# Attention weights of one of two source blocks on GpSimd instead of VectorE, with a new split of the squares

## The chip, the cores and the metric

The kernel runs on one core of a Trainium2 chip. The metric is the device time of one execution in microseconds (us). Each timed kernel ran several times, in rounds with the kernel before on the same chip. DVE is VectorE, ACT is ScalarE, POOL is GpSimd, PE is TensorE.

## The reference, cut to what matters

Four graph layers follow each other on 3327 nodes with 64 features. The change touches only the last one, a hyperbolic attention layer:

```
left = x_tan @ att_W[:D] + att_b
right = x_tan @ att_W[D:]
adj_att = jax.nn.sigmoid(left + right.T) * adj           # 3327 x 3327
x_local = _logmap(x[:, None, :], x[None, :, :], C)
support_t = jnp.einsum('ij,ijd->id', adj_att, x_local)
```

The kernel never builds `x_local`. For each pair (source, target) it needs a weight, (1 + tanh(.)) * adj, which is twice the sigmoid, and a scalar function of the distance, which it fits by a Gelu and the square of that Gelu plus a constant. Their product is contracted with the source nodes on PE.

## The kernel before

The layer goes over 26 pairs. A pair is two source blocks of 128 nodes (b = 0, 1) against half of the targets (HN = 1664). So a pair's tiles `gl` and `th` are 128 x 3328. `SQ` is the column at which the squares are divided between ACT (below it) and DVE (from it on).

```
SQ = HN + 512                                   # 2176
...
    def distances(n, k):        # half k of the columns of both blocks
        ...                     # 8 matmuls into the tiles pts[0], pts[1]
        for b in range(2):
            S.activation(gs[n][:, b, ...], pts[b], AF.Gelu, scale=-HA)
        S.activation(ths[n][:, k, :], leftb, AF.Tanh, bias=righth, scale=0.5)

    def squares(n):
        S.activation(gl[:, :SQ], gl[:, :SQ], AF.Square, bias=hg)
        V.scalar_tensor_tensor(gl[:, SQ:], gl[:, SQ:], 2 * HG, gl[:, SQ:], op0=OP.add, op1=OP.mult)

    def weights(n):
        th, a = ths[n], adjs.pop(n)
        for b in range(2):
            V.scalar_tensor_tensor(th[:, b, :], th[:, b, :], 1.0, a[:, b, :], op0=OP.add, op1=OP.mult)

    def products(n):
        for lo, hi, hd in ((0, HN, HD), (HN, SQ, HD), (SQ, 2 * HN, HD + HG * HG)):
            V.scalar_tensor_tensor(gl[:, lo:hi], gl[:, lo:hi], hd, th[:, lo:hi], op0=OP.add, op1=OP.mult)
    ...
    for n in range(-2, len(pairs)):
        if n >= 0: products(n)
        if 0 <= n + 1 < len(pairs): distances(n + 1, 1)
        if n >= 0: gather(n)                    # PE: accx, columns in four chunks of 416 a block
        if 0 <= n + 1 < len(pairs):
            weights(n + 1); load3(n + 3); squares(n + 1)
        if n + 2 < len(pairs):
            begin(n + 2); distances(n + 2, 0)
        if n >= 0: gather_p(n)                  # PE: accp
```

(Cut: helpers, the other layers, and the collection of a half.) Each engine takes its instructions in the order in which this loop issues them.

## Time and profile before

| | before |
|---|---|
| median of the first 3 runs | 920.91 us (920.04 to 924.06) |
| one pair of layer 3, steady | 8.63 us |
| DVE in the steady stretch | busy 80.00 of 80.00 us |
| ACT, POOL in that stretch | 76.34 us, 0 us |

The table is for a stretch of layer 3 in which nothing but the 26-pair loop runs. It is read from the busy times in that window, and the period is the distance between two equal instructions in the timeline. The prediction shows those lines. One view that it does not show is the timeline of ACT (start, length, engine, line, operation, shapes, count; idle time before it and what ended it):

```profile
696.47 1.62 ACT L818 ACTIVATE gl<-pt 128x832 f32<-128x832 f32 x2 [0.37 <-PE pt L810]
697.98 1.68 ACT L825 ACTIVATE th<-leftb,righth 128x1664 f32<-128x1664 f32 x1
```

The reader sees that ACT waits 0.37 us for PE's distances in each pair. PE in turn waits for ACT's Gelu before it may overwrite a distance tile.

### The profile page before, as it was taken

To read this page: it belongs to the slowest core of one execution; us is meant where nothing else is said; L and a number is where in the kernel's file an instruction comes from. 1 tells how busy PE (TensorE), PEld (TensorE's weight loads), DVE (VectorE), ACT (ScalarE), POOL (GpSimd) and SP (SyncE) were. 2 spreads that over 40 slices of the span, in tenths; PEclk is the share of its full clock that TensorE was granted. 3 is DMA by queue.
4 is the path that set the end of the run, shared out by engine and by line. 5 is a ranking of instruction groups with operands and counts; after the bars stand their busy time and mean duration, and the time that the engine had idled before them with its cause. 6 is when DMAs were issued, how large, how long until landed. Compare 5 with 4: busy or idle time off the path is not lost.

```text
span 920.6 us, 9670 instructions
## 1 busy us (share of the span) xinstructions
PE 720.2 (78%) x4043; PEld 339.6 (37%) x4043; DVE 519.6 (56%) x618; ACT 356.3 (39%) x361; POOL 9.5 (1%) x18
## 2 busy tenths in 40 slices
PE   0999998998953999505999999115899997699970
PEld 0644445443431444203444445112344442244420
DVE  4200025000189000796676675862899998899986
ACT  0000011000022000111666665012899995799961
POOL 1000000000000000000000002000000000000000
PEclk9999999999985999856999999556999997899995
DMA  8999930997000599500688610300465562445501
GB/s 274 378 379 429 404 122 21 384 359 275 0 1 0 209 385 373 221 0 1 253 330 310 243 53 1 151 3 10 149 223 176 197 222 80 159 159 217 200 24 22
DMA packets 25345, 170.22 MB, mean 185 GB/s; under 512 B 9165, under 2 KB 9293, under 8 KB 16077
## 3 DMA queue, kind: packets, MB, share of 16 engines
q1 hardware_dynamic: 21718, 168.88, 48.1%
q10 hardware_dynamic: 3575, 0.64, 0.4%
q8 instruction: 33, 0.54, 0.2%
q14 instruction: 19, 0.16, 0.1%
HBM read 168.40 MB, written 0.85 MB: 184 GB/s over the span
## 4 chain that ended last, share of the span: by engine, by line
PE 62%; DVE 19%; DMA 10%; issue 4%; ACT 3%; ACTq 1%; POOL 0%; SPq 0%; DVEq 0%; POOLq 0%
PE acc L261 28%; PE pt L799 9%; PE accx L870 8%; DMA adj<-in_adjT 6%; PE cnt L450 4%; PE cnt L458 4%; PE accp L885 3%; DMA res<-in_adjT 3%; PE pt L810 2%; DVE sq L86 1%; DVE gl L854 1%; PE lin L245 1%; ACT gl L818 1%; DVE n L88 1%; DMA w<-in_W 1%
## 5 line engine op out<-in xcount | busy, mean ns | idle before, releaser
L261 PE MATMUL acc<-adj,m_n 128*64 128x416 f32 x816 | 203.8, 523 | 9.4 <-DMA adj<-in_adjT 8.8
L261 PEld LDWEIGHTS acc<-adj,m_n 128*64 128x64 f32 x816 | 85.4, 138 | 109.7 <-issue 90.3
L261 PE MATMUL acc<-res,m_n 128*64 128x416 f32 x432 | 108.0, 523 | 22.8 <-DVE m_n L349 22.2
L466 ACT ACTIVATE w<-cnt,ebias 128x832 uint16<-128x832 f32 x104 | 93.4, 950 | 62.9 <-PE cnt L458 51.8
L278 DVE COPY m_t<-acc 128x416 f32<-128x416 f32 x12 | 6.2, 582 | 189.1 <-PE acc L261 189.1
L845 DVE SCALAR_TENSOR_TENSOR th<-th,adj 128x1664 f32<-128x1664 f32 x52 | 97.7, 1887 | 12.5 <-ACT th L825 12.4
L799 PE MATMUL pt<-xs 64*128 64x416 f32 x208 | 99.4, 559 | 5.4 <-ACT gl L818 5.4
L799 PE MATMUL pt<-xw,xs 64*128 64x416 f32 x208 | 100.5, 565 | 0.0
L854 DVE SCALAR_TENSOR_TENSOR gl<-gl,th 128x1664 f32<-128x1664 f32 (+2 forms) x78 | 97.6, 1305 | 0.0
L870 PE MATMUL accx<-gl,xd 128*64 128x416 f32 x416 | 83.2, 539 | 13.8 <-DVE gl L854 13.8
L818 ACT ACTIVATE gl<-pt 128x832 f32<-128x832 f32 x104 | 84.1, 861 | 24.3 <-PE pt L810 24.3
L825 ACT ACTIVATE th<-leftb,righth 128x1664 f32<-128x1664 f32 x52 | 87.6, 1685 | 0.0
L450 PE MATMUL cnt<-mask,tri 128*128 128x416 bf16 x208 | 70.8, 344 | 2.4 <-ACT w L466 1.0
L261 PEld LDWEIGHTS acc<-res,m_n 128*64 128x64 f32 x432 | 44.5, 138 | 68.4 <-issue 66.5
L261 PE MATMUL acc<-w,part 128*64 128x416 bf16 x624 | 66.1, 346 | 4.3 <-DVE part L413 4.3
L458 PE MATMUL cnt<-behind,ones 128*128 128x416 bf16 x192 | 65.1, 339 | 0.0
L476 DVE TENSOR_TENSOR behind<-behind,mask 128x3328 bf16<-128x3328 bf16 x23 | 43.5, 1892 | 36.0 <-PE cnt L458 36.0
L217 PE MATMUL tr<-ident,h_n 128*128 128x128 f32 x26 | 6.0, 423 | 62.4 <-DVE h_n L139 62.4
L836 ACT ACTIVATE gl<-gl,hg 128x2176 f32<-128x2176 f32 x26 | 54.8, 2106 | 0.0
L870 PEld LDWEIGHTS accx<-gl,xd 128*64 128x64 f32 x416 | 30.8, 141 | 62.1 <-DVE gl L854 33.4
L810 PE MATMUL pt<-rows_i,rows_j 64*128 64x416 bf16 x208 | 50.8, 347 | 0.0
L443 DVE TENSOR_SCALAR mask<-adj 128x3328 bf16<-128x3328 f32 x21 | 39.5, 1885 | 19.9 <-DMA adj<-in_adjT 13.3
(228 smaller groups left out, 645.4 us busy)
## 6 DMA issues: line engine op xcount, KB each, us to landing
adj<-in_adjT SPq DMA_DIRECT2D x89, 1664.0 KB
res<-in_adjT SPq DMA_DIRECT2D x9, 1664.0 KB
xn<-in_x SPq DMA_DIRECT2D x1, 832.0 KB
out<-w SPq DMA_DIRECT2D x2, 416.0 KB
ih<-in_wihT ACTq DMA_DIRECT2D x4, 48.0 KB
hh<-in_whhT ACTq DMA_DIRECT2D x4, 48.0 KB
w<-in_W ACTq DMA_DIRECT2D x4, 16.0 KB
attw<-in_att_W SPq DMA_DIRECT2D x1, 64.0 KB
```

The source lines that it names most:

```text
L261: T.matmul(acc[q][h * D : (h + 1) * D, :CH], lhsT=lhsT, rhs=rhs, start=first, stop=last)
L450: T.matmul(p[:, i, :CH], lhsT=tri, rhs=mask[:, i0 : i0 + CH], start=True, stop=behind is None,)
L458: T.matmul(p[:, i, :CH], lhsT=ones, rhs=behind[:, i0 : i0 + CH], start=False, stop=True,)
L466: S.activation(w, p[:, :, :CH], AF.Relu, bias=ebias, scale=-EXP_UNIT)
L799: T.matmul(pts[b][:, i, :CH], lhsT=xs[rs, c * P : (c + 1) * P], rhs=rhs[rs, q0 : q0 + CH], start=True, stop=False,)
L810: T.matmul(pts[b][:, i, :CH], lhsT=rows_j[rs, j0 : j0 + P], rhs=rows_i[rs, i0 : i0 + CH], start=False, stop=True,)
L818: S.activation(gs[n][:, b, 2 * k * CH : (2 * k + 2) * CH].rearrange("p (i n) -> p i n", i=2), pts[b][:, :, :CH], AF.Gelu, scale=-HA,)
L825: S.activation(ths[n][:, k, :], leftb[:, hf * HN : (hf + 1) * HN], AF.Tanh, bias=righth[:, kk : kk + 1], scale=0.5,)
L836: S.activation(gl[:, :SQ], gl[:, :SQ], AF.Square, bias=hg)
L845: V.scalar_tensor_tensor(th[:, b, :], th[:, b, :], 1.0, a[:, b, :], op0=OP.add, op1=OP.mult)
L854: V.scalar_tensor_tensor(gl[:, lo:hi], gl[:, lo:hi], hd, th[:, lo:hi], op0=OP.add, op1=OP.mult)
L870: T.matmul(acc[i // 2][(i % 2) * D : (i % 2 + 1) * D, :CH], lhsT=xd[:, c, b, :], rhs=gl[:, b, i * CH : (i + 1) * CH], start=first, stop=last,)
```

## The change

The intent is to take one of the two weights instructions off DVE, the full engine, and give it to POOL, which is idle. As DVE would then have room, part of the squares moves from ACT to DVE.

```
-SQ = HN + 512
+SQ = 1280
...
-        def weights(n):
-            th, a = ths[n], adjs.pop(n)
-            for b in range(2):
-                V.scalar_tensor_tensor(th[:, b, :], th[:, b, :], 1.0, a[:, b, :], op0=OP.add, op1=OP.mult)
+        def weights(n, b):
+            th, a = ths[n][:, b, :], adjs[n][:, b, :]
+            if b == 0:
+                G.tensor_scalar(th, th, 1.0, None, op0=OP.add)
+                G.tensor_mul(th, th, a)
+            else:
+                V.scalar_tensor_tensor(th, th, 1.0, a, op0=OP.add, op1=OP.mult)
+                adjs.pop(n)
...
-            for lo, hi, hd in ((0, HN, HD), (HN, SQ, HD), (SQ, 2 * HN, HD + HG * HG)):
+            for lo, hi, hd in ((0, SQ, HD), (SQ, 2 * HN, HD + HG * HG)):
...
-                weights(n + 1)
+                weights(n + 1, 1)
...
                 distances(n + 2, 0)
+                weights(n + 2, 0)
```

(Long lines are joined.)

More of the change, by code (lines that the diff above doesn't have):

```diff
@@ L839, in squares @@
             )
-        def weights(n):
-            th, a = ths[n], adjs.pop(n)
-            for b in range(2):
-                V.scalar_tensor_tensor(
-                    th[:, b, :], th[:, b, :], 1.0, a[:, b, :], op0=OP.add, op1=OP.mult
-                )
+        def weights(n, b):
[6 more added lines that the diff above has]
+                adjs.pop(n)
         def products(n):
```

## The prediction

> **What bounds the kernel now.** Layer 3 alone is changed, so I read the busy time per engine for a steady stretch of it, then the groups of that stretch by shape, then the timeline of VectorE and of ScalarE, then the chain of waits. The steady stretch first (columns: stretch, its length, busy us and instructions of each engine, granted clock, DMA share, GB/s):
>
> ```profile
> 660.00:740.00 80.00, 80.00 (x518) 34.52 (x519) 80.00 (x57) 76.34 (x66) 0.00 (x0) 1.00 0.57 203
> ```
>
> PE and DVE are busy for all of it, ACT for 95%, POOL not at all, at full clock. A busy PE is not a PE at its peak, so this row alone does not choose between PE and DVE. The groups by shape give the durations (busy us, mean ns of one, idle time before it):
>
> ```profile
> L845 DVE SCALAR_TENSOR_TENSOR th<-th,adj 128x1664 f32<-128x1664 f32 x18 | 33.9, 1887 | 0.0
> L825 ACT ACTIVATE th<-leftb,righth 128x1664 f32<-128x1664 f32 x19 | 32.0, 1685 | 0.0
> L818 ACT ACTIVATE gl<-pt 128x832 f32<-128x832 f32 x38 | 30.8, 861 | 3.7 <-PE pt L810 3.7
> ...
> L836 ACT ACTIVATE gl<-gl,hg 128x2176 f32<-128x2176 f32 x9 | 18.9, 2105 | 0.0
> L854 DVE SCALAR_TENSOR_TENSOR gl<-gl,th 128x1664 f32<-128x1664 f32 x10 | 18.8, 1883 | 0.0
> ...
> L854 DVE SCALAR_TENSOR_TENSOR gl<-gl,th 128x1152 f32<-128x1152 f32 x10 | 13.5, 1349 | 0.0
> ...
> L837 DVE SCALAR_TENSOR_TENSOR gl<-gl 128x1152 f32<-128x1152 f32 x9 | 12.2, 1351 | 0.0
> ...
> L854 DVE SCALAR_TENSOR_TENSOR gl<-gl,th 128x512 f32<-128x512 f32 x10 | 6.8, 682 | 0.0
> ```
>
> Every DVE group has no idle time before it: DVE is back to back. The timeline of DVE gives the period (start, length):
>
> ```profile
> 689.19 3.77 DVE L845 SCALAR_TENSOR_TENSOR th<-th,adj 128x1664 f32<-128x1664 f32 x2
> 692.88 1.35 DVE L837 SCALAR_TENSOR_TENSOR gl<-gl 128x1152 f32<-128x1152 f32 x1
> 694.15 3.75 DVE L854 SCALAR_TENSOR_TENSOR gl<-gl,th 128x1664 f32<-128x1664 f32 x3
> 697.82 1.88 DVE L845 SCALAR_TENSOR_TENSOR th<-th,adj 128x1664 f32<-128x1664 f32 x1
> ```
>
> One pair takes 697.82 - 689.19 = 8.63 us. The six durations are 2 x 1.887 + 1.351 + 1.883 + 0.682 + 1.349 = 9.04 us, so neighbours overlap by (9.04 - 8.63)/6 = 0.07 us. DVE is the full engine, and there are 26 pairs: 224 us of the 921.
>
> The chain of waits shows how near the others are:
>
> ```profile
> 694.39 1.94 PE pt L799 x8
> 696.34 0.27 PE pt L810
> 696.60 2.96 PE accx L870 x16
> ```
>
> The chain runs along PE all the time. PE's own work per pair is two distance halves of 1.95, the gather of 2.96 and the accp products of 1.51: 8.37 us. The second distance half takes 2.2 us instead of 1.95, because its second tile waits for ScalarE's Gelu. ACT steps in 4 x 0.75 + 2 x 1.57 + 2.00 = 8.14 us, with an idle 0.37 a pair. So DVE 8.63, PE 8.37, ACT 8.14: three engines within 6%, and relieving DVE alone can gain 0.26 us a pair before PE is the limit.
>
> **What the Trainium skill says.** "GPSIMD Engine Reference", section "Elementwise — side-by-side cycle accounting", measures a two-input fp32 tensor_tensor of 2048 columns at 4497 ns on GpSimd against 2293 ns on DVE, and says that one-input bodies run near one element a cycle. The trace has no two-input POOL operation. It has one copy:
>
> ```profile
> L670 POOL COPY xd<-xd 128x832 f32<-128x832 f32 x1 | 0.9, 879 | 23.7 <-DVE xd L665 23.7
> ```
>
> 879 ns for 832 columns agrees with one element a cycle plus about 0.19 us.
>
> "SBUF — State Buffer", section "Who interferes with whom": "A DVE instruction with two SBUF inputs contends with a GpSimd instruction that reads SBUF". The same section says that the shared pair is taken exclusively, whoever starts first keeping it for the whole instruction. The trace of before cannot confirm it: the single POOL copy, at 593.87 us, fell in a gap of DVE. "Perfetto Trace Analysis", section "Optimizing Scalar/DVE Operations", draws the conclusion that moving work between these two engines might not help.
>
> **The change part by part.**
> (1) Removed from DVE: one weights instruction a pair, 1.887 - 0.07 = 1.82 us.
> (2) The squares' boundary moves from 2176 to 1280. The slope of the DVE durations is (1.887 - 1.351)/512 = 1.046 ns a column, so DVE's square of 2048 columns takes 1.887 + 384 x 0.001046 = 2.29 us instead of 1.35: +0.94. ACT's square falls by 896 x (2105 - 1685)/512 ns = 0.74 us.
> (3) The products are cut in two (1280 and 2048 columns, 1.48 and 2.29 us) instead of three; less 0.07 for one instruction fewer they come to 3.63 against 3.71.
> New DVE sum: 1.887 + 2.29 + 1.48 + 2.29 - 4 x 0.07 = 7.67 us, 0.96 less. New ACT sum: 7.40 us.
> (4) Added to POOL: a one-input add of 1664 columns, 0.19 + 2 x 0.69 = 1.57 us (twice the columns of the copy at its rate), and a two-input multiply, estimated from the skill's figure as 4497 x 1664/2048 = 3.65 us. Sum 5.2 us a pair on an engine that was idle.
> (5) Waits: the first Tanh of pair n+2 ends about 1.9 us after the products of pair n+1 began, and the products of n+2 begin 8.6 us after those. POOL thus has some 6.7 us for 5.2: hidden if it runs undisturbed, with a slack of 1.5 us. The adjacency block is then needed up to a period earlier; its loads use 57% of the DMA time, so I expect no wait there.
> (6) The gather's fourth column chunk of the first block (1248 to 1664) now crosses the boundary at 1280, so PE waits in order for the second product: 1.41 + 2.22 = 3.6 us after the products began, not 1.84. As DVE now has spare time, this eats at most 0.3 us.
>
> If POOL and DVE were independent, the period would be PE's 8.37 to 8.6, a gain of 0 to 0.26 x 26 = 7 us. But every one of DVE's four remaining instructions (weights, squares, both products) is a scalar_tensor_tensor with two SBUF inputs, and both POOL operations read SBUF. Under the lock they cannot overlap at all, and the sum is the period: 7.67 + 5.2 = 12.9 us, some 13.0 with two handovers. That is 4.3 us more for each of the 26 pairs, 112 us; a few pairs at the start, at the middle where the half is collected and at the end have gaps of DVE to use, so I take 24 of them: +104 us, 1024 us.
>
> **The rivals.**
> Independent engines: POOL runs beside DVE without either slowing. The attraction is that this needs nothing more than what the diff intends, and that the new sums, 7.67 and 7.40, are so well balanced that somebody computed them for it. Time 913 to 922. Against it is the skill's explicit sentence on just these operands. PE then bounds, which is why even this rival gives no 2%.
> Shared port, but by turns within the instructions: DVE's second input needs the port for 7.67 us, POOL's three operands for 3 x 1664 columns at 1.2 a ns = 4.2 us at the rate of the copy. The period would be between 10.3 (if DVE's stream left some of the port free) and 11.9: +44 to +85 us, 965 to 1006.
> Starvation: DVE's stream, always ready, keeps the port until it must itself wait for POOL's weights. POOL then runs while DVE idles. It shows as a long DVE wait instead of long instructions, but the sum is the same 13 us; 1024 to 1050 if the handover is slow, since POOL's dependent chain (Tanh, add, multiply) no longer starts early.
> A late POOL without a lock: if the multiply took 5.5 us or more instead of 3.65, its slack of 1.5 us would be gone and each pair would wait for it, but two pairs are in flight, so this adds tenths of a us a pair: 920 to 935.
>
> **Range and chances.** I give a contended port 78% (full lock or starvation about 60, by turns about 18), and independent engines with or without a late POOL the rest. A contended port is slower by over 2% in each form. The centre is the full lock's 1024. The range 955 to 1050 holds the shared and the full forms; it leaves out the independent rival on purpose, since between 935 and 955 I expect nothing. Chances: faster by over 2% 0.03, within 2% 0.19, slower 0.78.
>
> **What would show each step right or wrong.** In a steady stretch the period should be near 13 us, PE and ACT busy near 65%, at full clock. The groups by shape should show either the DVE instructions with means well over 1.887 us (weights) and 2.29 us (2048 columns), or an idle time of DVE before the products released by POOL; the POOL multiply well over 3.65 us would say that it waits inside its instruction. The ACT square of 1280 columns should take 1.37 us; if it does and the period is still near 13, the balance is not the cause. I am wrong if DVE's means stay and POOL takes about 5.2 us beside it: then the period is 8.4 to 8.6 and PE limits. I am also wrong in size if POOL's one-input add is much dearer than a copy.

## More of the kernel before

All runs that are compared are in the fast state. One run of one experiment was in the slow state; this is said where it comes up.

## The result, and the profile after

The changed kernel takes 1085.03 us (median of 4 runs, 1083.59 to 1087.15), the kernel before 922.48 us (4 runs) in the same comparison. The ratio is 1.176, with an interval of 1.172 to 1.181. Ratios here are the mean time of one kernel's fast runs over that of the other's fast runs of the same rounds, so they differ slightly from the quotient of the medians that are quoted. The loss was predicted, but not its size: 162.5 us, against 104 us in the prediction, whose range ended at 1050 us.

The busy times in a steady stretch of the changed kernel, with the columns as in the prediction (PE, PEld, DVE, ACT, POOL, clock, DMA, GB/s):

```profile
700.00:760.00 60.00, 41.29 (x216) 15.79 (x210) 49.68 (x16) 30.05 (x28) 38.07 (x8) 0.83 0.30 106
```

PE has fallen from 100% to 69% and ACT from 95% to 50%. DVE is at 83%, although it has fewer instructions. The groups by shape say why (busy us, mean ns of one, idle time before it and its releaser), from the stretch 660 to 860 us:

```profile
L845 POOL TENSOR_SCALAR th<-th 128x1664 f32<-128x1664 f32 x13 | 69.5, 5350 | 79.2 <-ACT th L825 79.2
...
L856 DVE SCALAR_TENSOR_TENSOR gl<-gl,th 128x2048 f32<-128x2048 f32 x13 | 54.1, 4162 | 0.0
L846 POOL TENSOR_TENSOR th<-th,adj 128x1664 f32<-128x1664 f32 x13 | 53.8, 4136 | 1.1
L837 DVE SCALAR_TENSOR_TENSOR gl<-gl 128x2048 f32<-128x2048 f32 x13 | 50.9, 3913 | 0.0
...
L856 DVE SCALAR_TENSOR_TENSOR gl<-gl,th 128x1280 f32<-128x1280 f32 x12 | 36.4, 3037 | 0.0
...
L848 DVE SCALAR_TENSOR_TENSOR th<-th,adj 128x1664 f32<-128x1664 f32 x13 | 24.5, 1885 | 30.2 <-ACT th L825 30.2
...
L836 ACT ACTIVATE gl<-gl,hg 128x1280 f32<-128x1280 f32 x12 | 16.3, 1359 | 0.0
```

ACT's shorter square takes its expected time, 1.36 us. DVE's 2048-column instructions, expected at 2.29 us, have means of 3.9 and 4.2 us. A mean hides that there are two kinds of instruction in it, so the next step is one instance of each. Four of DVE's from the timeline, and the POOL operations of the same moments:

```profile
706.33 1.89 DVE L848 SCALAR_TENSOR_TENSOR th<-th,adj 128x1664 f32<-128x1664 f32 x1 [5.16 <-ACT th L825]
708.14 5.82 DVE L837 SCALAR_TENSOR_TENSOR gl<-gl 128x2048 f32<-128x2048 f32 x1
713.88 4.60 DVE L856 SCALAR_TENSOR_TENSOR gl<-gl,th 128x1280 f32<-128x1280 f32 x1
...
718.40 5.78 DVE L856 SCALAR_TENSOR_TENSOR gl<-gl,th 128x2048 f32<-128x2048 f32 x1
```

```profile
702.83 4.41 POOL L845 TENSOR_SCALAR th<-th 128x1664 f32<-128x1664 f32 x1 [11.41 <-ACT th L825]
707.32 4.49 POOL L846 TENSOR_TENSOR th<-th,adj 128x1664 f32<-128x1664 f32 x1
711.79 6.44 POOL L845 TENSOR_SCALAR th<-th 128x1664 f32<-128x1664 f32 x1
718.31 3.72 POOL L846 TENSOR_TENSOR th<-th,adj 128x1664 f32<-128x1664 f32 x1
...
733.44 4.41 POOL L845 TENSOR_SCALAR th<-th 128x1664 f32<-128x1664 f32 x1 [11.41 <-ACT th L825]
```

Read the two side by side. POOL's multiply ends at 707.32 + 4.49 = 711.81. DVE's square, begun at 708.14, ends at 713.96, that is 2.15 us after POOL let go. Its 2048 columns at 1.046 ns (the slope in the prediction) are 2.14 us: it did all of them in that last part and stood blocked before. The last product is the same: POOL's multiply ends at 722.03, the product at 724.18. It works the other way too. POOL's second add starts at 711.79, when the square is about to take the port, and lasts 6.44 us instead of the 4.41 of an undisturbed one. Here DVE and POOL take turns, instruction by instruction.

The rhythm repeats every 733.44 - 702.83 = 30.61 us, and that is two pairs: 15.3 us a pair. DVE's account of one rhythm is: 2 x 7.67 = 15.3 us of its own work, 3.53 + 3.12 + 3.50 = 10.2 us blocked inside three instructions (each duration less the natural one, that is the one without a rival), and 5.16 us idle for the Tanh. They sum to 30.7. The idle part is a consequence: the blocked product holds up PE's gather, PE's distances stand behind the gather in PE's order, and ACT's Gelu and Tanh wait for those.

The chain of waits of the same rhythm shows this path, and one cost more (start, length, what):

```profile
703.24 2.94 PE accx L872 x16
706.18 0.90 PE pt L799 x4
...
718.40 5.79 DVE gl L856
...
724.23 3.23 PE accx L872 x10
727.47 1.62 PE pt L799 x4
```

After the wait PE is slower. Ten gather matmuls take 3.23 us, where sixteen took 2.94 before (ten of them 1.84), and four distance matmuls take 1.62 us instead of 0.90. The granted clock was 1.00 from 702.8 to 711.0 us and 0.70 from 724.2 to 727.4. In this rhythm that is 1.39 + 0.72 = 2.1 us on the chain, by estimate 27 us of the 162 if all 13 rhythms are alike. No run tested what lowers the clock.

POOL's rows also show the surprise. The add, 4.41 us with DVE idle for most of it, costs more than the multiply with its two inputs.

### The profile page after: what moved, and what is told of

Same layout as the page of the kernel before. It is cut to its first block, busy times and chain, and to the rows that moved or that the text cites. A ratio compares the mean times of both kernels' runs of the same rounds, so it can differ in the third digit from the quotient of the medians.

```text
span 1083.7 us, 9732 instructions
## 1 busy us (share of the span) xinstructions
PE 771.3 (71%) x4043; PEld 348.5 (32%) x4043; DVE 626.1 (58%) x566; ACT 339.4 (31%) x361; POOL 255.0 (24%) x70
## 4 chain that ended last, share of the span: by engine, by line
PE 54%; DVE 25%; DMA 9%; ACT 7%; issue 4%; ACTq 1%; SPq 0%; DVEq 0%; POOL 0%; POOLq 0%
PE acc L261 24%; PE pt L799 8%; PE accx L872 7%; DVE gl L856 7%; DMA adj<-in_adjT 7%; PE cnt L450 4%; PE cnt L458 3%; PE accp L887 3%; ACT gl L818 2%; ACT th L825 2%; DVE gl L837 1%; ACT gl L836 1%; PE pt L810 1%; DVE sq L86 1%; PE lin L245 1%
## 5 line engine op out<-in xcount | busy, mean ns | idle before, releaser
L872 PE MATMUL accx<-gl,xd 128*64 128x416 f32 x416 | 128.7, 683 | 130.5 <-DVE gl L856 130.5
L845 POOL TENSOR_SCALAR th<-th 128x1664 f32<-128x1664 f32 x26 | 138.8, 5338 | 205.6 <-ACT th L825 159.0
L856 DVE SCALAR_TENSOR_TENSOR gl<-gl,th 128x1280 f32<-128x1280 f32 (+1 forms) x52 | 171.6, 3338 | 0.0
L872 PEld LDWEIGHTS accx<-gl,xd 128*64 128x64 f32 x416 | 39.6, 171 | 211.9 <-DVE gl L856 158.8
L846 POOL TENSOR_TENSOR th<-th,adj 128x1664 f32<-128x1664 f32 x26 | 107.1, 4118 | 2.2
L799 PE MATMUL pt<-xs 64*128 64x416 f32 x208 | 101.7, 571 | 4.6 <-ACT gl L818 4.6
L837 DVE SCALAR_TENSOR_TENSOR gl<-gl 128x2048 f32<-128x2048 f32 x26 | 101.7, 3911 | 0.0
L848 DVE SCALAR_TENSOR_TENSOR th<-th,adj 128x1664 f32<-128x1664 f32 x26 | 53.9, 2073 | 64.0 <-ACT th L825 64.0
L476 DVE TENSOR_TENSOR behind<-behind,mask 128x3328 bf16<-128x3328 bf16 x23 | 43.5, 1892 | 36.0 <-PE cnt L458 36.0
```

The lines of the kernel that those rows point to most:

```text
L799: T.matmul(pts[b][:, i, :CH], lhsT=xs[rs, c * P : (c + 1) * P], rhs=rhs[rs, q0 : q0 + CH], start=True, stop=False,)
L845: G.tensor_scalar(th, th, 1.0, None, op0=OP.add)
L846: G.tensor_mul(th, th, a)
L872: T.matmul(acc[i // 2][(i % 2) * D : (i % 2 + 1) * D, :CH], lhsT=xd[:, c, b, :], rhs=gl[:, b, i * CH : (i + 1) * CH], start=first, stop=last,)
```

## The experiments

**Port theory:** a DVE instruction with two SBUF inputs and a POOL instruction that reads SBUF exclude each other, so their times add. **Chain theory:** POOL's work is simply too long between the Tanh and the products, in engines that take their instructions in order, and the port is a side effect. **Split theory:** the new division of the squares and products is the culprit.

In four runs a part of the weights is wrong. The comparison with the reference is too coarse to notice this part of layer 3.

### POOL busy, but not reading

```
-                G.tensor_scalar(th, th, 1.0, None, op0=OP.add)
-                G.tensor_mul(th, th, a)
+                for _ in range(6):
+                    G.memset(th[:, :1536], 0.5)
```

> The changed kernel with POOL's add and multiply replaced by six memsets of 1536 columns on the same tile, about 8.3 us of POOL work per pair behind the same Tanh and ahead of the same products, but reading nothing (the result is wrong on purpose). Port theory (a DVE instruction with two SBUF inputs and a POOL instruction that reads SBUF exclude each other): DVE's instructions keep their natural 1.89, 1.48 and 2.28 us, and the time is 915 to 940 us; up to 940 because 8 us of POOL lie in the chain from Tanh to the products, more than the 6.7 us that there are. Chain theory (the length of POOL's work behind the Tanh sets the period, whoever holds a port): the time stays near 1085 us.

Measured: 961.47 us, ratio 1.046. The groups by shape of DVE, 700 to 760 us:

```profile
L837 DVE SCALAR_TENSOR_TENSOR gl<-gl 128x2048 f32<-128x2048 f32 x7 | 16.0, 2285 | 0.0
L856 DVE SCALAR_TENSOR_TENSOR gl<-gl,th 128x2048 f32<-128x2048 f32 x6 | 13.7, 2285 | 0.0
L848 DVE SCALAR_TENSOR_TENSOR th<-th,adj 128x1664 f32<-128x1664 f32 x7 | 13.2, 1892 | 7.8 <-ACT th L825 7.8
...
L856 DVE SCALAR_TENSOR_TENSOR gl<-gl,th 128x1280 f32<-128x1280 f32 x6 | 9.0, 1493 | 5.8 <-POOL th L846 5.8
```

Every DVE instruction has its natural duration, with POOL busy 50 of the 60 us. Writes by POOL do not touch DVE; reads do. That is for the port theory. But 961 is 21 us above the end of the expected range, so something else costs time as well, and a part of it is visible: the first product waits for POOL, 5.8 us in 6.

### The same with four memsets, and with the old split

> As the run with six memsets, but four: 5.7 us of POOL work behind the Tanh, reading nothing (the result is wrong on purpose). Six cost 961 us, more than the 915 to 940 expected. If that was the length of the chain (8.6 us of POOL against a slack of 6.7), four fit in it and the time is 912 to 922 us, with PE as the bound, which is also what the intended relief of DVE is worth at most; if it was some contention with POOL's writes, the loss falls only in proportion, to 945 to 950 us.

Measured: 942.80 us (median of the three fast runs), ratio 1.023 (interval 1.016 to 1.029). The fourth run, the profiled one, was slow; the ratio leaves it out, and the profile is used only for the order of things. The shorter chain gave back about 19 us, but not the rest. The chain of waits of this run (start, length, what) shows where it goes:

```profile
711.21 2.28 DVE gl L837
713.49 0.07 DVE gl L856
713.55 1.25 issue
714.80 2.30 DVE gl L856
717.10 0.04 issue
717.14 0.91 PE accx L872 x3
```

L837 is DVE's square, now 2048 columns, and L856 its two products ("issue" here is the time of the first one). PE's gather stands at the end of all three. In the kernel before, the chain ran along PE. So the moved squares have become part of the path from the distances to the gather. If that is right, the old split must bring the time back:

```
-SQ = 1280
+SQ = HN + 512
...        (and the three products of before)
```

> As the run with four memsets (944 us), with the split of the squares and the three products of before. If those 24 us over before came from the split, which puts a 2048-column square and then a 2048-column product on DVE between the second Tanh and the gather, this is 910 to 922 us: what the relief of DVE is worth when POOL's work is free of the port. If they came from POOL's writes or its chain, it stays at 940 to 950 us.

Measured: 922.70 us against 918.56, ratio 1.007. The difference between this and the run before it, 20 us by the fast medians and 15 us by the ratios, is the split. The run is also worth a look for what it does not do. DVE is now relieved of a weights instruction, with no one at its port, and yet:

```profile
704.82 1.89 DVE L848 SCALAR_TENSOR_TENSOR th<-th,adj 128x1664 f32<-128x1664 f32 x1 [1.79 <-ACT th L825]
706.63 1.35 DVE L837 SCALAR_TENSOR_TENSOR gl<-gl 128x1152 f32<-128x1152 f32 x1
707.90 3.75 DVE L856 SCALAR_TENSOR_TENSOR gl<-gl,th 128x1664 f32<-128x1664 f32 x3
713.45 1.89 DVE L848 SCALAR_TENSOR_TENSOR th<-th,adj 128x1664 f32<-128x1664 f32 x1 [1.79 <-ACT th L825]
```

The period is 713.45 - 704.82 = 8.63 us, as before, and DVE now idles 1.79 us of it, almost exactly the 1.82 us taken off. Even with a free POOL there was nothing to win.

### Only the split

```
-SQ = HN + 512
+SQ = 1280
...        (the two products of the change; the weights stay on DVE)
```

> Only the split of the squares moves (1280 columns on ACT, the products in two instructions); the weights stay on DVE and POOL does nothing. DVE's sum is 2 x 1.887 + 2.29 + 1.48 + 2.29 - 5 x 0.07 = 9.48 us instead of 8.63, so both theories that blame POOL expect 0.85 x 26 = 22 us: 940 to 946 us. If the split and not POOL were the cause of the loss, it would be near 1085 us.

Measured: 942.77 us against 918.45, ratio 1.027. It is in the expected range: DVE is full and its sum is longer. The split alone is a small part of the 162 us.

### Only the joined products

In the kernel before, the first two products become one of 2176 columns.

> The kernel before with its first two products joined (2176 and 1152 columns), the other small part of the change. DVE saves one 0.07 us a pair, PE may start the gather 0.5 us later, which its slack before the gather covers: 917 to 925 us, the same as before for every theory.

Measured: 920.30 against 918.56 us, ratio 1.002 (interval 0.996 to 1.007). No effect is seen.

### POOL's weights with the old split

> POOL makes the weights of the first block as in the changed kernel, but the split of the squares and the three products are those of before. Port theory: DVE's natural work falls to 6.8 us a pair, POOL's stays, and their sum falls by 0.87 us: 1058 to 1070 us, a little faster than the changed kernel. Chain theory: POOL's chain is untouched and ACT's square is 0.74 us longer: 1085 to 1105 us.

Measured: 1045.80 us, ratio 1.144. The sign is that of the port theory, but the gain over the changed kernel is 39 us by the medians, about 30 by the ratios (1.176 and 1.144 of 922 us), and not 15 to 27. The difference of the two runs with four memsets, 15 to 20 us for the split alone, says that more than DVE's sum depends on the split; how the two add up in the two-pair rhythm I did not take apart.

### A read that nobody waits for

The sharpest test of port against chain: the kernel before, all its waits as they were, and an extra POOL instruction a pair.

```
             th, a = ths[n], adjs.pop(n)
+            G.tensor_mul(extra, a[:, 0, :], a[:, 1, :])
```

> The kernel before, unchanged, with one more POOL instruction a pair that nobody waits for: it multiplies the two adjacency blocks of the pair into a scratch tile as soon as they have landed, two SBUF inputs, 1664 columns, some 3.6 us. It is on no chain from the Tanh to the products. Port theory: every one of its 3.6 us is taken from DVE, which is full: up to 3.6 x 26 = 94 us, 1000 to 1015 us. Chain theory: 918 to 925 us, as nothing on the chain has changed.

Measured: 998.11 us against 918.56, ratio 1.089; 2 us below the expected range. That is 79.6/26 = 3.06 us a pair for an instruction whose result is thrown away, and the trace lists nobody who waited for it. (Its tile must be read before the next load may fill it, but DVE waits for no load in layer 3 of this trace.) The shortest of these multiplies took 3.69 us. DVE's instructions are stretched, the weights from 1.89 us and the square from 1.35 (groups, 700 to 740 us):

```profile
L847 DVE SCALAR_TENSOR_TENSOR th<-th,adj 128x1664 f32<-128x1664 f32 x7 | 18.9, 2716 | 2.0 <-ACT th L826 1.9
...
L838 DVE SCALAR_TENSOR_TENSOR gl<-gl 128x1152 f32<-128x1152 f32 x4 | 12.4, 3103 | 0.0
```

The chain theory has no place for this run.

This run also shows that the turns are not always instruction by instruction:

```profile
689.23 17.25 POOL L845 TENSOR_TENSOR extra<-adj 128x1664 f32<-128x1664 f32 x2 [10.48 <-DMA adj<-in_adjT]
```

```profile
695.71 7.22 DVE L847 SCALAR_TENSOR_TENSOR th<-th,adj 128x1664 f32<-128x1664 f32 x2
```

The first of these two multiplies takes 11.95 us, about 8 us more than the shortest. In those 8 us, until 697.59, six DVE instructions run back to back at their natural lengths; only the next one is blocked, with 5.27 us instead of 1.89. A stream of DVE can thus keep POOL waiting, as in the prediction's rival of starvation. What decides who is next is not shown.

### Half of the columns

POOL makes the weights of 832 columns of the first block; DVE makes the other 2496 in one instruction.

```
+HW = 832
...
+            if b == 0:
+                G.tensor_scalar(th[:, 0, :HW], th[:, 0, :HW], 1.0, None, op0=OP.add)
+                G.tensor_mul(th[:, 0, :HW], th[:, 0, :HW], a[:, 0, :HW])
+            else:                                # thf, af: th and adj as 128 x 3328, from HW on
+                V.scalar_tensor_tensor(thf, thf, 1.0, af, op0=OP.add, op1=OP.mult)
```

> POOL makes the weights of only the first 832 columns of the first block, DVE those of the other 2496 in one instruction. Port theory: the period is the sum again, DVE 8.5 us and POOL some 4.2 us less what they overlap, 12 to 12.9 us, so 1005 to 1030 us: close to the middle between before and after. Chain theory: POOL's 4.2 us fit in the 6.7 us there are, so the time falls to 920 to 930 us.

Measured: 978.65 us, ratio 1.066. Neither theory's range holds it: too slow by 49 us for the chain theory, too fast by 26 for the sum. In its timeline DVE's weights take 4.22 us (natural 2.76) and its second product 0.6 us more than its natural 2.28, so POOL keeps DVE from the port for about 2.1 us a pair. Its instructions last 2.55 + 2.47 = 5.0 us. POOL's duration is thus not the measure. Part of it may pass while POOL itself waits for DVE, and part of the add may be free of the port. The next three runs look at that.

### The add alone, the multiply alone, and two two-input operations

The multiply alone leaves out the add (wrong). The add alone gives the multiply of the first block back to DVE:

```
-                G.tensor_mul(th, th, a)
...
+                V.scalar_tensor_tensor(t0, t0, 0.0, a0, op0=OP.add, op1=OP.mult)
```

The third writes th*a + a:

```
-                G.tensor_scalar(th, th, 1.0, None, op0=OP.add)
                 G.tensor_mul(th, th, a)
+                G.tensor_add(th, th, a)
```

> POOL does only the multiply (the add of 1 is left out, the result is wrong on purpose). By the port theory the multiply holds DVE's second read port for its natural 3.6 us, so the period is 7.67 + 3.6 = 11.3 us and the time 980 to 995 us. A theory that only the length of POOL's work behind the Tanh counts expects 920 us, as 3.6 us fit in the 6.7 there are.

Measured: 1002.07 us, ratio 1.089; 7 us above the range. The total is near the sum of the port theory, but the timeline is not that sum:

```profile
715.78 1.96 DVE L847 SCALAR_TENSOR_TENSOR th<-th,adj 128x1664 f32<-128x1664 f32 x1 [5.20 <-ACT th L825]
...
719.87 7.20 DVE L855 SCALAR_TENSOR_TENSOR gl<-gl,th 128x1280 f32<-128x1280 f32 x2
```

```profile
696.79 4.04 POOL L845 TENSOR_TENSOR th<-th,adj 128x1664 f32<-128x1664 f32 x1 [4.88 <-ACT th L825]
712.28 3.72 POOL L845 TENSOR_TENSOR th<-th,adj 128x1664 f32<-128x1664 f32 x1 [11.45 <-ACT th L825]
720.88 4.04 POOL L845 TENSOR_TENSOR th<-th,adj 128x1664 f32<-128x1664 f32 x1 [4.88 <-ACT th L825]
```

The rhythm is again two pairs, 720.88 - 696.79 = 24.09 us. The multiply at 712.28 runs almost wholly while DVE idles. The one at 720.88 blocks the products for 7.20 - 3.68 = 3.5 us. So DVE's account is 15.3 of work, 3.5 blocked once in two pairs, and 5.2 idle for the Tanh. Blocked and idle time come to 8.7 us, not far from two multiplies (7.4 us): here the sum is nearly met by luck.

> POOL does only the add of 1; DVE multiplies both blocks as before (with 0 added for the first), so its own sum is 9.48 us. If the add holds the port for its whole 4.41 us, the period is 13.9 us and the time 1045 to 1055 us; if it lets the port go some 1.4 us before its end, as the products behind it suggest in the changed kernel, 12.5 us and 1010 to 1025 us; without any exclusion 940 to 950 us, as with the split of the squares alone.

Measured: 1029.15 us, ratio 1.117. It lies 4 us above the range for an early release and 16 below that for a full hold, and part of it is DVE's wait for the add (4.5 us in two pairs, by its timeline). The timing decides more clearly than the total. The two products of this run and the add beside them:

```profile
704.99 6.80 DVE L857 SCALAR_TENSOR_TENSOR gl<-gl,th 128x1280 f32<-128x1280 f32 x2
```

```profile
703.34 5.99 POOL L845 TENSOR_SCALAR th<-th 128x1664 f32<-128x1664 f32 x1 [4.21 <-ACT th L825]
```

The products take 6.80 us instead of 3.7, so they are blocked for 3.1 us, from 704.99 to about 708.1. The add ends only at 709.33. It had released DVE some 1.2 us before its end. That end is real: an earlier add of this run ends at 694.74 + 4.40 = 699.14, and the DVE instruction that waits for it starts at 699.17.

> The same weights by two two-input POOL operations (th*a, then + a) of some 3.6 us each, 7.2 us instead of 8.0. If POOL's whole durations add to DVE's, the period falls by 0.8 us: 1060 to 1068 us. If the one-input add frees the port 1.4 us early and the two-input ones do not, the exclusive time rises a little, from 6.9 to 7.2 us a pair: 1085 to 1100 us.

Measured: 1091.04 us, ratio 1.184, in the range for an early release and 23 us above the other. Two instructions that together are 0.7 us shorter, by their shortest durations, than the add and the multiply make the kernel no faster, which fits that they hold the port for all of it.

### A try at a version that beats both

The run with the old split said that ACT's and PE's loop holds the period. So both Tanhs of a pair are made early, where ACT had an idle 0.37 us, and the squares' boundary moves the other way, to take load off DVE:

```
-SQ = HN + 512
+SQ = HN + 704
...
-            kk = 2 * c + k
-            S.activation(ths[n][:, k, :], ...)
+            for b in range(2) if k == 0 else ():
+                kk = 2 * c + b
+                S.activation(ths[n][:, b, :], ...)
```

> The kernel before, with both Tanhs of a pair made early, behind the first pair of Gelus, so that ACT's path from the second Gelus to the next first ones is 1.57 us shorter, and with the squares' boundary moved towards ACT, from 2176 to 2368. By durations DVE falls to 8.43 us a pair, ACT rises to 8.30, PE stays at 8.37. If what holds the kernel at 8.62 is both DVE's sum and the loop of Gelu, Tanh, square, Gelu and PE's distances, both are relieved and the time falls by some 0.2 x 26 = 5 us: 912 to 917 us. If only one of them were the bound, either half of this would have done, and the time may gain less; a new wait of PE for the later second Gelus would leave it at 918 to 925.

Measured: 919.44 us against 921.08, ratio 0.9996 (0.996 to 1.004). There is no gain. The timelines of ACT and DVE in this run:

```profile
705.09 1.62 ACT L818 ACTIVATE gl<-pt 128x832 f32<-128x832 f32 x2 [0.18 <-PE pt L810]
...
713.70 1.62 ACT L818 ACTIVATE gl<-pt 128x832 f32<-128x832 f32 x2 [0.18 <-PE pt L810]
```

```profile
704.94 3.76 DVE L855 SCALAR_TENSOR_TENSOR gl<-gl,th 128x1664 f32<-128x1664 f32 x3 [0.17 <-ACT gl L837]
...
713.55 3.76 DVE L855 SCALAR_TENSOR_TENSOR gl<-gl,th 128x1664 f32<-128x1664 f32 x3 [0.18 <-ACT gl L837]
```

The period is still 713.70 - 705.09 = 8.61 us, and now both engines have slack. Only PE has none. PE's work of 8.37 us and a hand-over are left: ACT's two Gelus take 1.62 us after one distance half, while PE has only the 1.51 us of accp to do before it needs the second of the two tiles again. I read the remaining quarter of a us from this; no run took it away.

## Why the prediction was wrong

The direction and the mechanism were right, the size was not.

- **What bounds the kernel before.** The prediction called DVE the bound and gave 0.26 us a pair to be won. DVE was full, but not the bound alone: relieved of 1.8 us, it idled 1.79 us and the period stayed at 8.63 us. The step "three engines within 6%" saw the numbers, but not the loop between ACT and PE. After the change it expected full clock; the granted clock was 0.83, and PE's slower work after its wait (about 2.1 us in two pairs) was in no step.
- **The port.** "They cannot overlap at all" for the four DVE instructions was right in kind. POOL that only writes leaves DVE at 1892, 2285 and 1493 ns. POOL that reads stretches the same instructions to 5.8 us, and an unused read costs 80 us. The rivals of an independent POOL and of a port shared by turns within an instruction are excluded for these operations: the blocked square did all its work after POOL's multiply had ended. That two inputs on DVE's side are needed was not tested: no run gave DVE an instruction with one.
- **The term that failed** is step (4): the one-input add, "1.57 us (twice the columns of the copy at its rate)". The trace shows 4.41 us, 2.8 times as much. The multiply, estimated at 3.65, was right (shortest 3.69). With the measured add the sum of the prediction's own step becomes 7.67 + 4.41 + 3.69 = 15.8 us instead of 12.9, against a measured 15.3. The working had said that it would be wrong in size "if POOL's one-input add is much dearer than a copy", and gave it no room in the range.
- **The sum as a rule** is only roughly right. The add frees the port about 1.2 us before its end, POOL's own waiting is in its durations, and DVE idles 5.16 us in two pairs. These errors partly cancel, so that 15.8 is so near 15.3 is partly luck. For the half-width run, which lost 60 us, they did not cancel.
- **The slack of POOL and the split** (steps 5 and 6) were taken as harmless: "hidden if it runs undisturbed", "at most 0.3 us". Without any port conflict the split costs 15 to 20 us and a POOL chain of 8.6 us another 19 to 21. The rival of independent engines was thus set too low at 913 to 922 us for this split: four memsets gave 943.
- **The shares**, as far as runs show them: of 162 us, the split and the path through the gather are about 20 (ratio 1.023 with four memsets), the length of POOL's chain about another 20 (1.046 with six), and the rest, some 120 us, appears when POOL reads; PE's lower clock after its waits, an estimated 27 us, is within it. The parts do not simply add, so this is an order of size and no exact division.

## What to carry to other kernels

Before moving work from DVE to POOL, list the SBUF inputs of the DVE instructions that will run beside it. If they have two each and POOL reads SBUF, as here, much of the work is not moved but put in line, at POOL's longer duration. An engine that is busy all the time need not be the one that sets the period: a dummy that frees the engine at no cost (here a memset in place of the moved work) tells in one run what the relief can be worth at most. And an operation's cost on another engine should come from a measurement of that operation, not from a neighbour like a copy.

## What the Trainium skill lacked or had wrong

- "GPSIMD Engine Reference", section "Engine selection", calls one-input elementwise work on GpSimd "roughly line-rate". The copy agrees (879 ns for 832 columns), but the fp32 tensor_scalar add took 4.41 us for 1664 columns and at least 2.29 us for 832, more than the two-input multiply of the same size (3.69 and 1.94 us).
- "SBUF — State Buffer", section "Who interferes with whom", was right that DVE with two SBUF inputs contends with GpSimd's reads and not with its writes. That the one who is first keeps the pair for the whole instruction held for the multiply. It did not hold for the one-input add, which let DVE go on after about 3.1 us of its 4.4. Nor is the one that is blocked always next: one POOL multiply waited about 8 us behind six DVE instructions. A DVE instruction with one input was not tried.
- "Perfetto Trace Analysis", section "Identifying the Most-Contended Engine", tells the reader to optimize the engine with the highest occupancy first (TensorE it judges by other measures). Here DVE had 100%, and taking 1.8 us of 8.6 off it at no cost gave a ratio of 1.007: the chain of waits ran along PE, at the same period.
